# Cross attention of 32 batches on one core: warm-up products, two places of preparation work, and the last block of the output are changed

## The chip, the cores and the metric

The kernel runs on one core of a Trainium2 chip. The core has a matrix engine (TensorE, **PE** in the profile, with its weight loads as PEld), a vector engine (VectorE, **DVE**), a scalar engine (ScalarE, **ACT**), a general engine (GpSimd, **POOL**) and SyncE (**SP**), which here only issues transfers. PE writes its results into eight banks of PSUM (128 partitions by 512 floats each); everything else lies in SBUF. The metric is the device time of one execution, in microseconds; lower is better. The profile numbers times from the start of its span.

## What is computed

Inputs are x and y (32 batches of 256 channels by 1024 positions, float32), two weights of 256 by 256 for the energies and the values (`w_qk`, `w_v`), one for the output (`w_t`), and two biases. In the reference's words:

```python
x_q = jnp.einsum('oc,bcn->bno', w_qk, y)
x_k = jnp.einsum('oc,bcn->bon', w_qk, x)
x_v = jnp.einsum('oc,bcn->bon', w_v, x) + b_v[None, :, None]
energy = jnp.einsum('bnc,bcm->bnm', x_q, x_k)
attention = jax.nn.softmax(energy, axis=-1)
attention = attention / (1e-07 + attention.sum(axis=1, keepdims=True))
x_r = jnp.einsum('bcn,bnm->bcm', x_v, attention)
x_r = jax.nn.relu(jnp.einsum('oc,bcn->bon', w_t, x - x_r) + b_t[None, :, None])
return x + x_r
```

## The kernel before

**Weights are folded first.** Energies need only G = w_qk' w_qk, so the kernel makes G once (`pg`, line 169), multiplies it with x of a batch (`Keys`, tile `gx`) and that with y (`Energy`, tiles `pe`, `e`). The values take W = (w_t w_v)' with a minus sign: w_t is turned by four transposes on PE into the banks `pt` (line 179), copied to `wtT` by ACT, and multiplied with w_v into `pw` (line 184); `Values` multiplies x of a batch with the result into the tile `ut`. The bias of the values is a row `uc` = -(w_t b_v), made by `value_bias` (line 189): two copies on DVE (line 194) spread b_v over 128 columns (`bvb`), and PE multiplies them with wtT into `pb`. The same function has DVE make `fold`, a matrix for summing over positions, in four copies of 32 partitions (line 202).

**Every large product is a Strassen-like scheme of seven products.** `lefts` (line 145) prepares the left factors of a 256 by 256 weight: two ACT copies out of the banks and four sums on DVE (`gs`, `wtTs`, `wvtTs`). `summed` (line 218) prepares the right factors of x and y (`xs`, `ys`): for batch 0 with four POOL additions each, for later batches with accumulating transfers on POOL's queue, handed out as `steps`. `Seven` (line 245) holds the order of the seven products: p1, p5, p2, p6, p3, p7, p4, accumulated in three banks, with ACT copies in between and the four result blocks c11, c12, c22, c21 made by DVE (c21 by ACT). `Keys.factors` makes four more sums on POOL (`gt`), `Values.factors` another four (`us`). p4 adds into the bank from which c22 reads, so p4 waits for c22.

**A batch** is: for four tiles of 128 rows the seven energy products, with minima and maxima folded into the DVE instructions that make `e`, the exponentials on ACT, and sums over rows on DVE (`acc`); then the keys and values of the next batch; then the column sums (`part`, `pS`, `rc`) and the output (`Attention`). `Attention.run` (line 510) scales `e` (`normal`), makes the sums `et` of its quarters (`mix`; t1, t2, t3, t4) and runs the products in its order; `put` (line 490) adds x to a finished block and stores it; the block (1,0) is finished by ACT's relu, a DVE addition and a store (`c21`, line 497). The last products of a batch (`end`) are run inside the next batch's energies.

**Order.** `InOrder` (line 66) makes the calls that go through `pe`, `dve`, `act` and `pool` issue in the order in which the program makes them on that engine. Calls that go to `nc.vector`, `nc.scalar` or `nc.tensor` directly (in the head: the memset, the zero products, `lefts`, `value_weights`, `value_bias`) are placed by the framework's scheduler. [...]Transfers are issued by SP in the program's order, except the two biases (ACT's queue, lines 133 and 134) and the accumulating ones (POOL's).

**The head** (lines 129 to 143, 595 to 631): SP loads w_qk, x of batch 0, w_t, w_v and y; PE runs three products of zeros, 128 by 512, into a bank that nobody reads (lines 138 to 142), then G, then the keys of batch 0, w_t's turning, pw, pb, p4 of the keys, and the values of batch 0 through p4 (lines 617 to 628), and then the first energies.

**The tail** is the last batch's `run` with `before` set, and `finish` (line 553), which makes the last block in two halves of 256 columns: product, relu on ACT, addition on DVE, store, each half after the other.

Of the kernel before, what the change touches and what calls it, by code (L numbers as in the profile page):

```python
# [16 lines left out]
def kernel(  # L17
# [29 lines left out]
    nc = tc.nc  # L47
# [81 lines left out]
    nc.sync.dma_start(wqk, w_qk.rearrange("(k p) c -> p k c", p=P))  # L129
    load("x", 0, KC)  # L130
    nc.sync.dma_start(wt, w_t.rearrange("(k p) c -> p k c", p=P))
    nc.sync.dma_start(wv, w_v.rearrange("(k p) c -> p k c", p=P))
    nc.scalar.dma_start(bv, b_v.rearrange("(k p o) -> p k o", p=P, o=1))
    nc.scalar.dma_start(bt, b_t.rearrange("(k p o) -> p k o", p=P, o=1))
    load("y", 0)


    zeros = const.tile([P, MB], F32, name="zeros")
    nc.vector.memset(zeros, 0.0)
    idle = bank("idle")  # L140
    for _ in range(3):
        nc.tensor.matmul(idle, zeros[:, :P], zeros, start=True, stop=True)  # L142
    make_identity(nc, ident)

    def lefts(name, ps, sign=1.0):


        w = const.tile([P, KC, C], F32, name=name)
        for k in range(KC):
            nc.scalar.mul(w[:, k, :], ps[k][:, :C], sign)  # L150
        sums = const.tile([P, 4, P], F32, name=f"{name}s")
        s1, s2, s3, s4 = (sums[:, j] for j in range(4))

        def stt(out_, block, factor, other, op):
            nc.vector.scalar_tensor_tensor(out_, block, factor * sign, other, ALU.mult, op)

        p11, p12, p21 = ps[0][:, :P], ps[1][:, :P], ps[0][:, P:C]
        a11, a12, a21, a22 = w[:, 0, :P], w[:, 1, :P], w[:, 0, P:], w[:, 1, P:]
        stt(s1, p21, 1.0, a22, ALU.subtract)
        stt(s3, p11, 1.0, a21, ALU.subtract)  # L160
        stt(s2, p11, -1.0, s1, ALU.add)
        stt(s4, p12, 1.0, s2, ALU.add)
        return w, (a11, a12, s4, a22, s1, s2, s3)
# [2 lines left out]
    pg = [bank(f"pg_{i}") for i in range(KC)]  # L166
    for i in range(KC):
        for k in range(KC):
            nc.tensor.matmul(  # L169
                pg[i][:, :C], wqk[:, k, ts(i, P)], wqk[:, k, :], start=(k == 0), stop=(k == KC - 1)  # L170
            )
    _, g_left = lefts("g", pg, -1.0)

    def value_weights():

        pt = [bank(f"pt_{i}") for i in range(KC)]
        for i in range(KC):
            for k in range(KC):
                nc.tensor.transpose(pt[i][:, ts(k, P)], wt[:, k, ts(i, P)], ident)
        wtT, t_left = lefts("wtT", pt)  # L180
        pw = [bank(f"pw_{i}") for i in range(KC)]
        for i in range(KC):
            for k in range(KC):
                nc.tensor.matmul(  # L184
                    pw[i][:, :C], wv[:, k, ts(i, P)], wtT[:, k, :], start=(k == 0), stop=(k == KC - 1)
                )
        return wtT, t_left, lefts("wvtT", pw, -1.0)[1]

    def value_bias(wtT):

        bvb = scratch[:, 6, : KC * P].rearrange("p (k c) -> p k c", k=KC)
        pb = bank("pb")
        for k in range(KC):
            nc.vector.tensor_copy(bvb[:, k, :], bv[:, k, :].to_broadcast([P, P]))
            nc.tensor.matmul(  # L195
                pb[:, :C], bvb[:, k, :], wtT[:, k, :], start=(k == 0), stop=(k == KC - 1)
            )
        nc.scalar.mul(uc[:, 0, :], pb[:, :C], -1.0)
        nc.scalar.mul(nbt[:, :, 0], bt[:, :, 0], -1.0)

        for a in range(NG):
            nc.vector.tensor_copy(
                fold[ts(a, G32)],
                ident[ts(a, G32), ts(a, G32)].unsqueeze(1).to_broadcast([G32, NG, G32]),
            )
# [6 lines left out]
    def temp(tag, name):  # L212
        return cp.tile([P, MB], F32, tag=tag, name=name)
# [221 lines left out]
    class Attention(Seven):  # L435
# [27 lines left out]
                into, t_left[j - 1], self.xr[j - 1], start=not onto, stop=False, skip_group_check=True  # L463
            )

        def epart(self, into, j, tiles=range(HT), cols=slice(0, MB)):
            for t in tiles:
                pe.matmul(
                    into[:, cols],
                    self.ur[j - 1][:, t],  # L470
                    self.er[j - 1][:, t, cols],
                    start=False,
                    stop=(t == HT - 1),
                    skip_group_check=True,
                )
# [34 lines left out]
        def run(self, u, before=None):  # L510


            self.normal(0, 0)
            if u:
                u.c22()
            self.normal(1, 0)
            if before:
                before.put()
                before.c21()
            self.normal(0, 1)  # L520
            self.mix(self.t1, self.b11, self.b12, ALU.add)
            self.normal(1, 1)
            self.mix(self.t2, self.t1, self.b22, ALU.subtract)
            self.epart(self.one, 1)
            self.p1s = self.biased(self.one, "p1s", bt[:, 0, :])
            self.epart(self.three, 2)
            self.epart(self.two, 5)
            self.p5s = self.biased(self.two, "p5s", bt[:, 1, :])
            self.xpart(self.one, 6, True)
            if u:  # L530
                u.p4()
                u.c21()
                u.c11()
                u.c12()
            self.c11()
            self.put()
            self.xpart(self.two, 3, True)
            self.epart(self.two, 3, (0, 1))
            self.epart(self.one, 6)
            self.w = self.biased(self.one, "w", nbt[:, 0, :])  # L540
            self.mix(self.t3, self.b12, self.b22, ALU.subtract)
            self.mix(self.t4, self.b21, self.t2, ALU.subtract)
            self.epart(self.two, 3, (2,))
            if u:
                self.epart(self.two, 3, (3,))
                self.c12()
                self.put()
# [4 lines left out]

        def finish(self):

            self.xpart(self.one, 7, True)
            self.epart(self.one, 7)
            self.epart(self.two, 3, (3,))
            self.c22()
            self.put()
            self.c12()  # L560
            self.put()
            self.xpart(self.one, 4, True)
            z = temp("z", f"z_{self.b}_1_0")
            for cols in (ts(0, MB // 2), ts(1, MB // 2)):
                self.epart(self.one, 4, cols=cols)
                act.activation(
                    z[:, cols], self.one[:, cols], AF.Relu, bias=bt[:, 1, :], scale=1.0
                )
                dve.tensor_tensor(
                    z[:, cols], z[:, cols], loaded["x", self.b][:, 1, cols], ALU.add  # L570
                )
                nc.sync.dma_start(out[self.b, ts(1, P), cols], z[:, cols])

    def columns(b):

# [24 lines left out]
    g.p2()  # L600
    g.c11()
    g.p6()
    g.p3()
    g.c12()
    g.p7()
    g.c22()
    wtT, t_left, u_left = value_weights()
    value_bias(wtT)
    g.p4()
    g.c21()  # L610
# [13 lines left out]
    u.c12()  # L624
    u.p7()
    u.c22()
    u.p4()
    u.c21()
    u.bias()
    xsteps[1]()  # L630
    xsteps[2]()

    before = None
    for b in range(B):
# [3 lines left out]
        for t in range(HT):  # L638
            now = Energy(b, t, lhs, rhs)
            pair.append(now)  # L640
            now.p1()
            if t > 0:
                pair[t - 1].exp(1)
            now.p5()
            if t == 0:
                if before is not None and more:
                    before.end()
                    before.c21()
                    load("x", b + 1)
                e = ep.tile([P, NT, N], F32, tag="e", name=f"e_{b}")  # L650
                acc = one.tile([P, N], F32, tag="acc", name=f"acc_{b}")
                ur, usteps = u.factors()
            if t > 1:
                pair[t - 2].share(0)
            if t == 0:
                now.p6()
            now.p2()
            now.c11()
            if t == 1:
                pair[0].scale(1)  # L660
            if t > 1:
                pair[t - 1].share(1)
            if t > 0:
                now.p6()
            if t == 1:
                act.activation(acc, e[:, HT, :], AF.Copy, scale=scales[HT])
            if t > 0:
                pair[t - 1].p4()
                pair[t - 1].c21()
                pair[t - 1].exp(0)  # L670
            now.p3()
            now.c12()
            now.p7()
            now.c22()
            if t == 0:
                for step in usteps:
                    step()
                if more and b > 0:
                    xn, xsteps = summed("x", b + 1)
            elif more and b > 0:  # L680
                xsteps[t - 1]()
# [100 lines left out]
```

## Time and profile before

| what | value |
|---|---|
| median of 3 runs | 2153.83 us (2153.35 to 2154.16) |
| the profiled execution | 2153.93 us |
| its span | 2152.1 us |
| one batch in the steady state (start of the energies to the next) | 66.56 us |
| PE products of the head: zeros, from 1.45 us | G from 6.73, keys from 8.62, values from 18.60, energies from 25.94 |
| last product's first pass | 2142.81 us |
| DVE's last instruction | 2148.76 us, 0.42 us long |
| DMA | 131 GB/s on average over the span |

A float32 product appears in the profile as two records on PE, so "x8" are four products. [...]one of 512 columns lasts 592 ns, yet the next starts 0.43 us after it. The busy shares of the page are averages over 32 batches; the change touches only the first 30 us and the last 35, so the timeline of these windows is what to read. In a timeline the brackets at a line's end give the idle time of the engine before it and what ended it.

### The profile page before, as it was taken

How to read it: one execution, taken by the hardware profiler on the slowest of the kernel's cores; microseconds unless marked ns; L12 is line 12 of the kernel's file. 1: busy time of each engine (PE TensorE's matmuls, PEld its weight loads, DVE VectorE, ACT ScalarE, POOL GpSimd, SP SyncE). 2: the span in 40 equal slices, each digit the busy share in tenths (PEclk: the TensorE clock that was granted, in tenths of full speed). 3: DMA queues.
4: the chain of work that ended last, by engine and by line, in shares of the span. 5: the costliest groups of instructions: out<-in, count | busy, mean ns of one | idle time of the engine just before them, and what ended most of it. 6: DMA issues, size and time to landing. Idle time of an engine off the chain costs nothing.

```text
span 2152.1 us, 19871 instructions
## 1 busy us (share of the span) xinstructions
PE 2143.6 (100%) x6374; PEld 1064.0 (49%) x6374; DVE 1803.4 (84%) x2964; ACT 788.5 (37%) x1322; POOL 597.4 (28%) x488
## 2 busy tenths in 40 slices
PE   9999999999999999999999999999999999999998
PEld 5555445555445545455544555545554445544453
DVE  5898888898888988889888898888888888988897
ACT  4224432344432344323443234442244422444332
POOL 4322223322233223232232321323222233222320
PEclk9999999999999999999999999999999999999999
DMA  6555665556655556665566654665546655566640
GB/s 157 132 123 122 151 156 123 123 122 150 149 123 134 118 144 147 127 144 110 137 149 134 143 114 126 157 144 129 128 117 150 154 123 129 119 149 147 126 94 30
DMA packets 139192, 282.59 MB, mean 131 GB/s; under 512 B 9168, under 2 KB 42960, under 8 KB 139088
## 3 DMA queue, kind: packets, MB, share of 16 engines
q0 software_dynamic: 75936, 114.83, 33.9%
q1 hardware_dynamic: 62608, 166.48, 22.6%
q8 instruction: 51, 0.84, 0.2%
q14 instruction: 53, 0.43, 0.1%
q10 hardware_dynamic: 544, 0.00, 0.0%
HBM read 181.67 MB, written 33.55 MB: 100 GB/s over the span
## 4 chain that ended last, share of the span: by engine, by line
PE 98%; DVE 1%; issue 0%; ACT 0%; DVEq 0%
PE po L77 44%; PE pe L77 35%; PE pu L77 9%; PE pg L77 9%; DVE e L77 1%; PE idle L142 0%; DVE acc L77 0%; PE pS L77 0%; PE pw L184 0%; PE pg L169 0%; DVE z L77 0%; DVE rc L77 0%; DVE et L77 0%; ACT z L77 0%; PE pb L195 0%
## 5 line engine op out<-in xcount | busy, mean ns | idle before, releaser
L77 PE MATMUL pe<-gt,ys 128*128 128x512 f32 x768 | 392.2, 592 | 0.0
L77 DVE SCALAR_TENSOR_TENSOR e<-e,ri,rc 128x512 f32<-128x512 f32 x512 | 348.6, 743 | 1.1
L77 PE MATMUL po<-et,us 128*128 128x512 f32 x768 | 345.4, 592 | 1.2 <-DVE et L77 1.2
L77 DVE SCALAR_TENSOR_TENSOR acc<-e,ri,acc 128x1024 f32<-128x1024 f32 x224 | 288.9, 1290 | 8.0
L77 PE MATMUL pe<-gx,y 128*128 128x512 f32 x512 | 261.4, 592 | 0.0
L77 DVE TENSOR_TENSOR et<-e 128x1024 f32<-128x1024 f32 x128 | 254.0, 2022 | 0.0
L77 PEld LDWEIGHTS pe<-gt,ys 128*128 128x128 f32 x768 | 145.8, 190 | 184.2 <-issue 178.4
L77 PEld LDWEIGHTS po<-et,us 128*128 128x128 f32 x768 | 144.3, 190 | 187.0 <-issue 186.1
L77 PE MATMUL po<-e,ut 128*128 128x512 f32 x512 | 224.9, 593 | 0.0
L77 POOL TENSOR_TENSOR gt<-gx 128x512 f32<-128x512 f32 x64 | 101.7, 1589 | 433.2 <-DVE gx L77 433.2
L77 ACT COPY ep1s<-pe 128x512 f32<-128x512 f32 x128 | 75.0, 586 | 301.8 <-PE pe L77 285.1
L77 ACT ACTIVATE e<-e,nm 128x1024 f32<-128x1024 f32 x128 | 147.1, 1149 | 98.5 <-DVE nm L77 97.0
L77 PEld LDWEIGHTS po<-e,ut 128*128 128x128 f32 x512 | 97.3, 190 | 122.5 <-issue 94.5
L77 PEld LDWEIGHTS pe<-gx,y 128*128 128x128 f32 x512 | 97.2, 190 | 122.0 <-issue 114.1
L77 DVE CUSTOM_DVE_ANT_0 e<-pe,ep1s 128x512 f32<-128x512 f32 x128 | 88.5, 691 | 78.9 <-ACT e L77 62.8
L77 DVE TENSOR_TENSOR z<-z,x 128x512 f32<-128x512 f32 (+1 forms) x33 | 22.3, 676 | 149.7 <-ACT z L77 149.7
L77 ACT ACTIVATE e<-e,bias 128x1024 f32<-128x1024 f32 x128 | 147.4, 1151 | 0.5 <-DVE bias L77 0.5
L77 POOL DMA_DIRECT2D ut<-uc x32 | 50.5, 1579 | 313.2 <-DVE ut L77 258.3
L77 PE MATMUL pe<-gx,ys 128*128 128x512 f32 x256 | 130.9, 593 | 0.4 <-DVE nm L77 0.4
L77 PE MATMUL pe<-gt,y 128*128 128x512 f32 x256 | 130.7, 592 | 0.0
L77 POOL TENSOR_TENSOR us<-ut 128x512 f32<-128x512 f32 x64 | 82.6, 1291 | 149.1 <-DMA ut<-uc 149.1
L77 PE MATMUL po<-e,us 128*128 128x512 f32 x256 | 120.5, 592 | 0.0
(112 smaller groups left out, 3250.1 us busy)
## 6 DMA issues: line engine op xcount, KB each, us to landing
y<-in_ctx_dram SPq DMA_DIRECT2D x32, 1024.0 KB, 4.9
ut<-uc POOLq DMA_DIRECT2D x32, 1024.0 KB, 9.7
out_dram<-z SPq DMA_DIRECT2D x127, 256.0 KB, 2.0
x<-in_x_dram SPq DMA_DIRECT2D x31, 1024.0 KB, 8.2
xs<-in_x_dram SPq DMA_DIRECT2D x62, 512.0 KB, 4.4
ys<-in_ctx_dram SPq DMA_DIRECT2D x62, 512.0 KB, 4.1
xs<-in_x_dram POOLq DMA_DIRECT2D x31, 512.0 KB, 9.1
xs<-xs POOLq DMA_DIRECT2D x31, 512.0 KB, 5.0
```

Of the source, the lines that this page charges most:

```text
L77: self.last = getattr(self.engine, name)(*args, **kwargs)
```

## The change

It does five things.

- The products of zeros become eight of 128 by 128, on a tile `few` of their own, cleared ahead of `zeros`.
- The two bias loads go to SP's queue: b_v between w_t and w_v, b_t between w_v and y.
- w_t's turning (`turned_weights`) is split from `value_weights` and stands between p6 and p3 of batch 0's keys; the copies that spread b_v (`spread_bias`) stand behind the keys' c22; `fold` stays in `value_bias`. All of this now goes through the ordered `pe`, `dve` and `act`, so that its place is the program's.
- p4 and c21 of batch 0's values, their bias transfer and two steps of batch 1's `xs` go behind the first two energy products of batch 0.
- In the last batch the previous batch's last `put` and `c21` go behind the sum t1, and the last block is made whole: one product sequence of 512 columns, one DVE instruction max(z, -b_t) + (x + b_t) that takes the bank, and one store. x + b_t is made earlier by ACT.

On the engines' queues this leaves the number of products the same except for the zeros (three become eight) and the last block (eight of 256 columns become four of 512).

```diff
     nc.sync.dma_start(wt, w_t.rearrange("(k p) c -> p k c", p=P))
+    nc.sync.dma_start(bv, b_v.rearrange("(k p o) -> p k o", p=P, o=1))
     nc.sync.dma_start(wv, w_v.rearrange("(k p) c -> p k c", p=P))
-    nc.scalar.dma_start(bv, b_v.rearrange("(k p o) -> p k o", p=P, o=1))
-    nc.scalar.dma_start(bt, b_t.rearrange("(k p o) -> p k o", p=P, o=1))
+    nc.sync.dma_start(bt, b_t.rearrange("(k p o) -> p k o", p=P, o=1))
     load("y", 0)
...
     zeros = const.tile([P, MB], F32, name="zeros")
-    nc.vector.memset(zeros, 0.0)
+    few = const.tile([P, P], F32, name="few")
+    dve.memset(few, 0.0)
+    dve.memset(zeros, 0.0)
     idle = bank("idle")
-    for _ in range(3):
-        nc.tensor.matmul(idle, zeros[:, :P], zeros, start=True, stop=True)
+    for _ in range(8):
+        pe.matmul(idle[:, :P], few, few, start=True, stop=True)
...
-    def value_weights():
+    def turned_weights():
 
         pt = [bank(f"pt_{i}") for i in range(KC)]
         for i in range(KC):
             for k in range(KC):
-                nc.tensor.transpose(pt[i][:, ts(k, P)], wt[:, k, ts(i, P)], ident)
-        wtT, t_left = lefts("wtT", pt)
+                pe.transpose(pt[i][:, ts(k, P)], wt[:, k, ts(i, P)], ident)
+        return lefts("wtT", pt)
+
+    def value_weights(wtT):
+
         pw = [bank(f"pw_{i}") for i in range(KC)]
...
+    def spread_bias():
+        for k in range(KC):
+            dve.tensor_copy(bvb[:, k, :], bv[:, k, :].to_broadcast([P, P]))
...
             self.normal(1, 0)
+            self.normal(0, 1)
+            self.mix(self.t1, self.b11, self.b12, ALU.add)
             if before:
                 before.put()
                 before.c21()
-            self.normal(0, 1)
-            self.mix(self.t1, self.b11, self.b12, ALU.add)
...
         def finish(self):
 
+            xb = temp("op1s", f"xb_{self.b}")
+            act.activation(
+                xb, loaded["x", self.b][:, 1, ts(0, MB)], AF.Identity, bias=bt[:, 1, :], scale=1.0
+            )
...
-            self.xpart(self.one, 4, True)
+            self.end()
             z = temp("z", f"z_{self.b}_1_0")
-            for cols in (ts(0, MB // 2), ts(1, MB // 2)):
-                self.epart(self.one, 4, cols=cols)
-                act.activation(
-                    z[:, cols], self.one[:, cols], AF.Relu, bias=bt[:, 1, :], scale=1.0
-                )
-                dve.tensor_tensor(
-                    z[:, cols], z[:, cols], loaded["x", self.b][:, 1, cols], ALU.add
-                )
-                nc.sync.dma_start(out[self.b, ts(1, P), cols], z[:, cols])
+            dve.scalar_tensor_tensor(z, self.one, nbt[:, 1, :], xb, ALU.max, ALU.add)
+            self.store(1, 0, z)
...
     g.p6()
+    wtT, t_left = turned_weights()
     g.p3()
     g.c12()
     g.p7()
     g.c22()
-    wtT, t_left, u_left = value_weights()
+    spread_bias()
+    u_left = value_weights(wtT)
     value_bias(wtT)
...
-    u.p4()
-    u.c21()
-    u.bias()
-    xsteps[1]()
-    xsteps[2]()
...
             if t == 0:
-                if before is not None and more:
+                if b == 0:
+                    u.p4()
+                    u.c21()
+                    u.bias()
+                    xsteps[1]()
+                    xsteps[2]()
+                elif more:
                     before.end()
```

More of the change, by code (lines that the diff above doesn't have):

```diff
@@ L149, in lefts @@
         for k in range(KC):
-            nc.scalar.mul(w[:, k, :], ps[k][:, :C], sign)
+            act.mul(w[:, k, :], ps[k][:, :C], sign)
         sums = const.tile([P, 4, P], F32, name=f"{name}s")
@@ L154, in stt @@
         def stt(out_, block, factor, other, op):
-            nc.vector.scalar_tensor_tensor(out_, block, factor * sign, other, ALU.mult, op)
+            dve.scalar_tensor_tensor(out_, block, factor * sign, other, ALU.mult, op)
         p11, p12, p21 = ps[0][:, :P], ps[1][:, :P], ps[0][:, P:C]
@@ L168 @@
         for k in range(KC):
-            nc.tensor.matmul(
+            pe.matmul(
                 pg[i][:, :C], wqk[:, k, ts(i, P)], wqk[:, k, :], start=(k == 0), stop=(k == KC - 1)
@@ L183, in value_weights @@
             for k in range(KC):
-                nc.tensor.matmul(
+                pe.matmul(
                     pw[i][:, :C], wv[:, k, ts(i, P)], wtT[:, k, :], start=(k == 0), stop=(k == KC - 1)
                 )
-        return wtT, t_left, lefts("wvtT", pw, -1.0)[1]
+        return lefts("wvtT", pw, -1.0)[1]
+    bvb = scratch[:, 6, : KC * P].rearrange("p (k c) -> p k c", k=KC)
+    def spread_bias():
+        for k in range(KC):
+            dve.tensor_copy(bvb[:, k, :], bv[:, k, :].to_broadcast([P, P]))
     def value_bias(wtT):
-        bvb = scratch[:, 6, : KC * P].rearrange("p (k c) -> p k c", k=KC)
         pb = bank("pb")
         for k in range(KC):
-            nc.vector.tensor_copy(bvb[:, k, :], bv[:, k, :].to_broadcast([P, P]))
-            nc.tensor.matmul(
+            pe.matmul(
                 pb[:, :C], bvb[:, k, :], wtT[:, k, :], start=(k == 0), stop=(k == KC - 1)
             )
-        nc.scalar.mul(uc[:, 0, :], pb[:, :C], -1.0)
-        nc.scalar.mul(nbt[:, :, 0], bt[:, :, 0], -1.0)
+        act.mul(uc[:, 0, :], pb[:, :C], -1.0)
+        act.mul(nbt[:, :, 0], bt[:, :, 0], -1.0)
         for a in range(NG):
-            nc.vector.tensor_copy(
+            dve.tensor_copy(
                 fold[ts(a, G32)],
@@ L464, in xpart, with epart @@
             )
-        def epart(self, into, j, tiles=range(HT), cols=slice(0, MB)):
+        def epart(self, into, j, tiles=range(HT)):
             for t in tiles:
                 pe.matmul(
-                    into[:, cols],
+                    into,
                     self.ur[j - 1][:, t],
-                    self.er[j - 1][:, t, cols],
+                    self.er[j - 1][:, t],
                     start=False,
```

## The prediction

> **What bounds the kernel now.** I read the page's head and its chain of waits first. The span is 2152.1 us of the profiled execution's 2153.93 us; the runs' median is 2153.83, so the sum below is made in the span and moved over unchanged (0.1 us apart).
>
> ```profile
> span 2152.1 us, 19871 instructions
> PE 2143.6 (100%) x6374; PEld 1064.0 (49%) x6374; DVE 1803.4 (84%) x2964; ACT 788.5 (37%) x1322; POOL 597.4 (28%) x488
> PE 98%; DVE 1%; issue 0%; ACT 0%; DVEq 0%
> ```
>
> PE carries the whole chain. Thirty of the 32 batches are untouched and repeat every 66.56 us, so the change can win only where PE stands or runs slowly: before batch 0's energies and in batch 31's tail. First the tail, in the chain by time (start, length, what), and the timeline behind its last part (start, length, engine, idle before it):
>
> ```profile
> 2115.99 4.72 DVE e L77 x7
> 2120.71 1.20 DVE z L77 x2
> 2121.91 1.39 DVE e L77 x3
> ...
> 2124.57 1.15 DVE et L77
> 2125.71 0.14 issue
> 2125.85 19.83 PE po L77 x48
> ```
> ```profile
> 2142.81 1.12 PE L77 MATMUL po<-xs,wtT 128*128 128x512 f32 x2
> 2143.77 1.89 PE L77 MATMUL po<-et,ut 128*128 128x256 f32 x8
> 2146.22 1.99 PE L77 MATMUL po<-et,ut 128*128 128x256 f32 x8 [0.56 <-ACT z L77]
> ```
>
> Read: two z instructions of DVE lie on the path to the sum (et) that PE awaits, and the second half of the last block waits for ACT to read the first. Now the head: the timeline of PE, then the groups by tile (count: ns min/median/max, first to last start):
>
> ```profile
> 15.04 1.99 PE L184 MATMUL pw<-wtT,scratch 128*128 128x256 f32 x8 [0.25 <-ACT wtT L150]
> 24.94 1.16 PE L77 MATMUL pu<-wvtT,xs 128*128 128x128 f32 x8 [0.78 <-DVE ut L77]
> ```
> ```profile
> L142 PE MATMUL idle<-zeros x6: 1061/1061/1219, 1.5 to 5.9; 128*128 128x512 f32 x6
> L202 DVE COPY fold<-scratch x4: 218/1093/1283, 9.8 to 12.5; 32x128 f32<-32x128 f32 x4
> L194 DVE COPY scratch<-scratch x2: 221/224/227, 4.8 to 5.0; 128x128 f32<-128x128 f32 x2
> ```
>
> Read: a product is two records (passes). The zero passes start 0.853 us apart and last 1061 ns; the same form lasts 592 ns later: they run at half clock. PE waits for wtT and for ut. And the fold copies last five times as long as the like-sized bias copies of line 194, which ran while POOL was idle.
>
> **The tail.** (1) The two z instructions (1.20 us) move behind the sum t1. PE's product before it is through at 2124.46 (last start 2124.04 + 0.43), t1's first half would be there 1.20 us earlier, so PE starts at 2124.65 instead of 2125.85: **1.20 us**. DVE's total stays, so t2 still ends at 2129.40 + 2.35 = 2131.75; PE wants its first half at 2133.04 - 1.20 = 2131.84. Tight, but met; t3 (2135.35, wanted at 2137.17) has room. (2) The last block whole: from 2142.81 to the end of DVE's last instruction (2148.76 + 0.42) are 6.37 us. After: 0.96 to the first pass of e, 8 passes at 0.43, 0.16 for the last one's end, then one instruction out of the bank, 0.69 by the z row of that shape: 5.26 us. Saves 1.11. Its store is 256 KB (2.0 us to landing in the page) instead of 128 KB (1.7): -0.27. The added x + bias on ACT lies in the 8.3 us in which ACT idles before its last relu. Tail: 1.20 + 0.84 = **2.0 us** (1.5 to 2.2, if the store lands as slowly as the 2.3 of the last window, or as fast as 1.7).
>
> **The head, to the first product.** The first memset shrinks from 512 to 128 columns: from 0.485 us to between 0.20 (POOL's of that size) and 0.485; I take 0.28, so PE starts at 1.24 instead of 1.45. Sixteen passes of a quarter of 0.853 us take 3.41; with 0.16 of filling they end at 4.81. w_qk lands at 0.74 + 3.9 = 4.64, so PE does not stand. G's products thus start 1.92 us earlier than 6.73, but still cold: their starts (6.73, 7.11, 7.33) put the switch to full clock at about 7.05. Five and a quarter of the eight passes run at 0.427 instead of 0.216; they end at 7.64 instead of 8.62: **0.98**. Here a rule weighs. The Trainium skill (TensorE: Matmul & The Clock Gate, Part 1: The HAM clock gate) says that full clock comes after a window of about 3.4 us of sustained activity, at a phase of its own. The row shows 5.6 us from first pass to switch; the rule would allow 3.4 to 6.8. By the row the gain is 0.98, by the rule's earliest switch about 1.9. I keep the row. The b_v and b_t loads leave ACT's queue for SP's (0.49 and 0.50 us to issue); w_v, y and x of batch 1 issue up to 1 us later behind them, but y's packets had waited for the DMA engines anyway (issued 3.65, landed 12.4), so nothing.
>
> **w_t's turning** goes between p6 and p3. Before, from its first pass to pw's were 0.85 us, 0.41 of them waiting for ACT's wtT; now p3 and p7 (1.7 us) cover that: **0.45** with the small wait in p7. DVE now does wtT's sums ahead of c12 and c22. pb could start at 16.88 - 1.43 = 15.45.
>
> **The bias copies are the doubtful step.** They move from 4.81, where they cost nothing, to behind c22, so to about 15.0 on DVE; pb waits for them, and p4, the values and everything on PE behind pb. POOL runs ys and gt there without a gap from 12.43 to 22.54, 1.24 us each. Row: with POOL idle such a copy takes 224 ns; the fold copies beside POOL took 1093 to 1283, each ending when POOL's instruction ended. The rule that speaks against the change is the Trainium skill's (SBUF — State Buffer, Who interferes with whom): DVE copies in two-port mode and POOL lock each other out for a whole instruction. By the idle row, pb starts at 15.45 and the head gains 2.6; by the rule and the fold rows the first copy waits half an instruction (0.62) and the second, as POOL stands ready again, a whole one: 15.0 + 0.62 + 1.24 + 0.2 = 17.05, pb at 17.2. That is 0.35 later than before, and eats all of the 1.43. I take this, since the fourth fold copy, issued right behind the third, let POOL's ys in between. The fold copies themselves come after wvtT's sums, from 18.1 to at most 23.2, when POOL's stream ends; c11, c12, c22 of u follow by 25.0.
>
> **The values' last product** goes behind the energies' first two. Before, PE stood from 24.00 to 24.94 for c22, and 0.13 for ACT ahead of the energies' third product. From u's first product to the energies' third were 9.19 us, now 5.40 + 1.72 + 0.90 = 8.02: **1.17**; it is wanted at 26.1, c22 is there at 25.0. What pays: u's copy on ACT now follows two energy copies, so the bias DMA on POOL, and behind it in POOL's queue xs's two steps and the four us instructions, come at 40.5 instead of 39.7, while PE is 0.8 earlier. DVE's sums (acc) meet these: 1.44 and 2.21 us instead of 1.28, and DVE has no slack from 40.1 to 51.3 by the chain. Relative to them us moves by 1.6 us: between -1.1 (none meets) and +1.3 (two sums wait a whole POOL instruction); I take **-0.4**, nearer to what is there.
>
> **Sum.** Head: -0.35 + 1.17 - 0.4 = 0.4. Tail 2.0. Total 2.4 us: span 2149.7, **time 2151.4 us**.
>
> **Rivals.** *The copies slip in* (0.27): both get in at one boundary or meet none; pb at 15.5 to 16. Head 1.7 to 2.6, total 3.7 to 4.6: about 2149.6. For it: 224 ns at 4.81; against: the fold rows. *The clock comes a window late* (0.10): the shorter zeros leave a hole before w_qk or count for less; full clock at 10.4 instead of 7.05 costs half of 3.4 us: 2153.1. Against: PE is busy without a hole by the sum. *POOL keeps the port* (0.10), the slower side: at 2076.93 one et sum of DVE lasted 4533 ns where its twin took 1210, waiting over both of POOL's gt instructions in a row. If a copy loses at every boundary, pb waits for the stream's end, 22.6: values 5.8 us late, head -4.6, total -2.6: 2156.5, more if PE cools down. It decides from the fourth boundary lost (two more cost 2.7 us); against it: each fold copy got in at the next boundary. *The ends don't bring it* (0.05): t2 late or the store slow, tail 0.8: 2152.6.
>
> **Chances and range.** Forecast 0.48. The measurement tells from no change about 0.2%, 4.3 us, that is times below 2149.5 or above 2158.1. Faster beyond it needs the free copies and more: 0.20; slower beyond it needs the kept port and a cold PE: 0.04; the rest 0.76. The range, 2149.0 to 2153.3, leaves out the kept port and the extreme of the free copies.
>
> **What would show it.** Zero passes ending near 4.8 and G's first passes still 0.43 apart; pb's start (15.5 or 17.2) and DVE's two copies before it (0.2 or over 1 us each); no wait of u's last product for ut; the et wait at 2125.85 gone; one last store, DVE ending 5.3 us after the last block's first pass. I am wrong if pb waits not at all, or if the energies' first stall, 0.17 us at 51.37 before, grows beyond 1 us.

## The result, and the profile after

The changed kernel takes **2149.82 us** (median of 20 runs, 2147.97 to 2150.94), the kernel before on the same chips 2153.76 us (20 runs, 2152.73 to 2154.33): a ratio of 0.9982, 95% interval 0.9975 to 0.9989, or 3.9 us. The forecast was 2151.4, with a range from 2149.0 to 2153.3. What the forecast did not have is the spread: 3.0 us over the runs of the changed kernel, 1.6 over those of the one before. The experiments had to explain that too.

The profiled execution took 2150.47 us, its span is 2148.7. The head of the page, and the line of the chain's shares by engine:

```profile
span 2148.7 us, 19867 instructions
PE 2141.6 (100%) x6376; PEld 1063.8 (50%) x6376; DVE 1806.6 (84%) x2964; ACT 788.0 (37%) x1321; POOL 597.4 (28%) x488
PE 98%; DVE 1%; DMA 0%; issue 0%; POOL 0%; ACT 0%; SPq 0%; DVEq 0%; POOLq 0%
```

Nothing changes in the large, as the steady batches are the same; but DMA and POOL, which were not in the old chain's shares, are in this one. The chain of the first 30 us says where (start, length, what):

```profile
1.73 6.56 DMA x<-in_x_dram
...
8.43 1.28 POOL xs L77
...
9.75 1.14 PE pg L77 x2
...
14.37 2.22 DVE scratch L77 x2
16.59 0.04 issue
16.63 0.70 PE pb L77 x2
17.33 0.86 PE pg L77 x2
18.19 5.41 PE pu L77 x48
23.59 1.72 PE pe L77 x4
25.31 0.89 PE pu L77 x8
26.20 3.86 PE pe L77 x9
```

The head is now held at two places: x's second half with POOL's sum of it ends just ahead of the keys' p6 (9.75), and DVE's two bias copies, 2.22 us of them, end just ahead of pb (16.63). The keys' p4 (17.17) stands behind pb in PE's queue and so begins behind it, though it uses nothing of pb, and c22, for which it has to wait, ended at 14.37. Ahead of the energies' third product nothing waits any more: four passes, the values' last product (eight), and on. The same in the timeline of PE (start, length, operation; in brackets PE's idle time and what ended it):

```profile
1.05 3.79 PE L77 MATMUL idle<-few 128*128 128x128 f32 x16 [1.05 <-DVE few L77]
4.63 2.15 PE L77 MATMUL pg<-scratch 128*128 128x256 f32 x8
6.62 1.02 PE L77 MATMUL pg<-x,g 128*128 128x512 f32 x2
...
15.41 0.70 PE L77 MATMUL pb<-wtT,scratch 128*128 128x256 f32 x2 [0.65 <-DVE scratch L77]
16.63 0.70 PE L77 MATMUL pb<-wtT,scratch 128*128 128x256 f32 x2 [0.52 <-DVE scratch L77]
```

And in the tail, the timeline of PE and then that of all engines:

```profile
2123.02 3.67 PE L77 MATMUL po<-et,us 128*128 128x512 f32 x8
```
```profile
2144.64 0.75 DVE L77 SCALAR_TENSOR_TENSOR z<-po,nbt,xb 128x512 f32<-128x512 f32 x1 [2.66 <-PE po L77]
2145.42 0.33 SPq L492 DMA_DIRECT2D out_dram<-z  x1
```

PE starts on `et` without a bracket, that is without waiting, and one DVE instruction and one store end the kernel.

For the next table, G in PE's timeline before:

```profile
6.73 2.05 PE L169 MATMUL pg<-scratch 128*128 128x256 f32 x8
```

How far the changed kernel is ahead of the old one, at points of the two profiles:

| point | before | after | ahead by |
|---|---|---|---|
| G's first pass | 6.73 | 4.63 | 2.10 |
| keys' p1 (G is through) | 8.62 | 6.62 | 2.00 |
| keys' p6 | 11.47 | 9.75 | 1.72 |
| pw | 15.04 | 12.87 | 2.17 |
| values' p1 | 18.60 | 18.03 | 0.57 |
| energies' p6 | 27.78 | 26.04 | 1.74 |
| first pass of pS, batch 0 | 59.33 | 57.68 | 1.65 |
| first pass of pS, last batch | 2113.09 | 2111.46 | 1.63 |
| end of the last z on DVE | 2149.19 | 2145.39 | 3.80 |
| end of the span | 2152.1 | 2148.7 | 3.4 |

The head brings 1.65 us of this, the tail 1.8.

### The profile page after: what moved, and what is told of

It is laid out like the page before. It is cut to its first block, busy times and chain, and to the rows that moved or that the text cites. A ratio compares the mean times of both kernels' runs of the same rounds, so it can differ in the third digit from the quotient of the medians.

```text
span 2148.7 us, 19867 instructions
## 1 busy us (share of the span) xinstructions
PE 2141.6 (100%) x6376; PEld 1063.8 (50%) x6376; DVE 1806.6 (84%) x2964; ACT 788.0 (37%) x1321; POOL 597.4 (28%) x488
## 4 chain that ended last, share of the span: by engine, by line
PE 98%; DVE 1%; DMA 0%; issue 0%; POOL 0%; ACT 0%; SPq 0%; DVEq 0%; POOLq 0%
PE po L77 45%; PE pe L77 35%; PE pu L77 9%; PE pg L77 9%; DVE e L77 0%; DMA x<-in_x_dram 0%; DVE acc L77 0%; PE pS L77 0%; DVE scratch L77 0%; POOL xs L77 0%; DVE gx L77 0%; DVE wtTs L77 0%; DVE z L77 0%; PE pb L77 0%; ACT gw L77 0%
## 5 line engine op out<-in xcount | busy, mean ns | idle before, releaser
L77 DVE TENSOR_TENSOR z<-z,x 128x512 f32<-128x512 f32 x31 | 21.5, 693 | 145.7 <-ACT z L77 145.7
```

The source lines that it names most:

```text
L77: self.last = getattr(self.engine, name)(*args, **kwargs)
```

## The experiments

Theory: the zeros and the point at which PE's rate doubles set when G is through; DVE's bias copies take turns with POOL; each part of the tail is worth what it was priced at. Rival theories stand in each expectation, mostly of the form "something else holds this place anyway". Each kernel is the changed one with the edit shown. The profiles also serve as repeated samples of what was not edited. In the text, g and u are the keys and the values of batch 0, and "u's p1" is the first product of the values. Experiments 3 to 7 ran once each, so only stretches of their profiles are read, not their times.

Two things were not tried: the bias loads back in ACT's queue, and DVE's copies at their old early place. There they took 0.36 us at 4.81, as soon as b_v had landed (4.0 us after its issue at 0.74) and with POOL idle; in the changed kernel b_v lands 6.6 us after its issue at 2.68.

**1. The bias copies on ACT.**

```diff
-            dve.tensor_copy(bvb[:, k, :], bv[:, k, :].to_broadcast([P, P]))
+            act.copy(bvb[:, k, :], bv[:, k, :].to_broadcast([P, P]))
```

> The changed kernel with the two bias copies made by ACT in place of DVE, nothing else. Theory (DVE's two copies, 14.29 to 16.58 in the changed kernel, take turns with POOL's sums of y, and PE's pb stands behind them): ACT's copies run at some 0.3 to 0.4 us each whatever POOL does, pb follows pw at once at about 14.6 instead of 15.41 and 16.63, the keys' p4 begins at about 15.7 instead of 17.17, and the start of every later stage moves by 1.4 to 1.6 us: pS at about 56.4, span about 2147.2, if the granted clock rises at the same point as in the changed kernel's profile. Rival (POOL's sums for y and the keys hold the first energies anyway, so the wait only moves): p4 is early, but the first energy e.p6 stays within 0.3 us of 26.04 and the span of 2148.7.

2148.37 us (7 runs, 2147.39 to 2148.75; ratio to before 0.9974, 0.9963 to 0.9985), span 2146.4. Group and timeline of that profile:

```profile
L77 ACT COPY scratch<-scratch x2: 308/314/319, 11.6 to 11.8; 128x128 f32<-128x128 f32 x2
```
```profile
12.56 1.89 PE L77 MATMUL pw<-wtT,scratch 128*128 128x256 f32 x8
14.29 1.03 PE L77 MATMUL pb<-wtT,scratch 128*128 128x256 f32 x4
15.15 1.02 PE L77 MATMUL pg<-xs,g 128*128 128x512 f32 x2
16.01 1.05 PE L77 MATMUL pu<-wvtT,x 128*128 128x128 f32 x8
```

ACT makes a copy in 0.31 us, pb follows pw with no bracket, and from pw's first pass to the values' p1 are 3.45 us instead of 5.16: 1.71 for the copies. The values, energies and pS all keep it; the rival falls. In this profile ACT makes the copies between 11.62 and 12.13, while POOL is idle until 13.90; that ACT is not held up beside POOL is shown by experiments 8 and 9 alone, where its copies run beside POOL's sums of y and take 0.29 to 0.30 us each. In 8:

```profile
11.80 1.27 POOL L77 TENSOR_TENSOR ys<-y 128x512 f32<-128x512 f32 x1 [0.57 <-DMA y<-in_ctx_dram]
12.20 0.50 ACT L77 COPY scratch<-scratch 128x128 f32<-128x128 f32 x2 [0.57 <-DMA scratch<-in_L_xattn_b_v_dram]
```

By pS this kernel is 2.30 ahead of the profile after: 0.31 of that came before pw (POOL's sum of x began 0.51 earlier, and p6 0.20), 1.71 from the copies, and 0.28 later, from a stall in the energies that is missing here.

**2. The old zeros.** Three products of 512 columns again:

```diff
-    few = const.tile([P, P], F32, name="few")
-    dve.memset(few, 0.0)
...
-    for _ in range(8):
-        pe.matmul(idle[:, :P], few, few, start=True, stop=True)
+    for _ in range(3):
+        pe.matmul(idle, zeros[:, :P], zeros, start=True, stop=True)
```

> The changed kernel with the kernel before's three products of 512 zero columns in place of the eight of 128, nothing else. Theory (the end of the zeros and the clock's rise set where G ends): G begins at about 6.7 instead of 4.63 and ends at 7.6 to 8.6 instead of 6.62, by where the granted clock rises; p6 no longer waits for POOL's sum and begins at 10.4 to 11.5 instead of 9.75, and 0.7 to 1.7 us are left of that at pS (58.5 to 59.5). Rival (the head's gain comes from w_t's turning and the loads, not from the zeros, since POOL's second sum of x holds p6 in any case): p6 moves by less than 0.4 us, and pS stays within 0.4 us of 57.85.

2151.66 us (10 runs; ratio 0.999, 0.9981 to 1.0). G begins at 6.30, ends at 8.03, p6 is at 10.88, pS at 58.34, 0.66 later than after. Against the kernel before on its own chip this one gains 2.0 us, the changed kernel 3.9: by the medians the zeros are worth 1.9, about half of the whole. The two intervals overlap, but eight of the ten runs lie above all twenty of the changed kernel. The rival falls on p6 (1.13 later, not under 0.4); pS lies between what theory and rival said for it, since this profile's copies cost 0.37 less.

Experiments 3 to 6 undo one part of the change each.

**3. The z steps at their old place.**

```diff
+            if before:
+                before.put()
+                before.c21()
             self.normal(0, 1)
             self.mix(self.t1, self.b11, self.b12, ALU.add)
-            if before:
-                before.put()
-                before.c21()
```

> The changed kernel with the last stage's two z steps of the batch before put back ahead of the second normalisation and the sum t1, nothing else. Theory: PE waits again for et in the last stage's second product, 1.2 us, so that the stretch from pS of the last batch to the last DVE instruction is 1.2 us longer (34.9 instead of 33.7) and the span with it. Rival (DVE has the same work in either order, so its end decides): within 0.3 us of 33.7.

The wait is back at its old length:

```profile
2123.23 3.67 PE L77 MATMUL po<-et,us 128*128 128x512 f32 x8 [1.21 <-DVE et L77]
```

From the first pass of pS, last batch, to the end of the last z: 35.13 us, against 33.93 in every other kernel with the whole last block made by one instruction. 1.20, as priced.

**4. The values' last product at its old place**, ahead of the energies.

```diff
     u.c22()
+    u.p4()
+    u.c21()
+    u.bias()
...
-                if b == 0:
-                    u.p4()
-                    u.c21()
-                    u.bias()
...
-                elif more:
+                if b > 0 and more:
```

> The changed kernel with the values' last product and what follows it put back ahead of batch 0's energies, nothing else. Theory: the product stands again for DVE's c22 (about 0.9 us) and the energies' third product again for ACT: from u's first product to the energies' p6 9.1 to 9.2 us instead of 8.01. POOL's bias DMA comes earlier again, so that the later sums of DVE meet the four us instructions elsewhere; if that cost the 0.4 us that was set down for it, the stretch from u's first product to pS grows by 0.8 only, and if nothing, by 1.17 (the two profiles at hand say 1.08: 40.73 before, 39.65 after).

From u's first product to the energies' p6: 9.19 instead of 8.01, with the old wait in PE's timeline:

```profile
22.79 1.16 PE L77 MATMUL pu<-wvtT,xs 128*128 128x128 f32 x8 [0.78 <-DVE ut L77]
```

1.18, as priced. To pS it grows by 1.70, more than either number expected: the stall of PE ahead of the last energies' p4 is 0.78 us here (0.17 before, 0.33 after). The step that I feared for POOL's later instructions goes the other way in this profile; in the twelve profiles with the new place that stall is 0.28 to 0.35 us nine times and missing three times.

**5. The last block in two halves**, as before.

```diff
-            self.end()
+            self.xpart(self.one, 4, True)
...
-            dve.scalar_tensor_tensor(z, self.one, nbt[:, 1, :], xb, ALU.max, ALU.add)
-            self.store(1, 0, z)
+            for cols in (ts(0, MB // 2), ts(1, MB // 2)):
+                self.epart(self.one, 4, cols=cols)
...
```

> The changed kernel with the last block again in two halves, each with its relu on ACT, its sum on DVE and its store, nothing else. Theory: the second half's products stand for ACT's read of the first half, 0.5 us, and relu and sum follow one after the other: from pS of the last batch to the end of DVE's last instruction 37.8 instead of 36.73 us; the last store is 128 KB instead of 256 KB and its end follows DVE's by 0.4 us less, so the span grows by 0.6 to 0.7 only against the same head. Rival (the store's size costs nothing): the span grows by the full 1.0.

In that expectation two scales are mixed: 36.73 reaches from pS to a point 0.5 us ahead of the span's end, not to the last z, which ends 33.93 behind pS. By the z, 34.89: 0.96 longer. By the span's end, 37.87 instead of 37.23: 0.64 longer. So the whole block saves 0.96 and its store, with twice the bytes, gives 0.33 back (3.31 us from z's end to the span's end instead of 2.98); the rival falls. Below, "the end" is the span's; the 36.5 to 36.7 of later expectations are 0.5 less for the same thing, and their 3.25 is 0.05 less.

**6. w_t's turning behind p7.**

```diff
-    wtT, t_left = turned_weights()
     g.p3()
     g.c12()
     g.p7()
     g.c22()
+    wtT, t_left = turned_weights()
     spread_bias()
```

> The changed kernel with w_t's turning put back behind p7, nothing else. Theory: from p6 to pw 3.57 us instead of 3.12 (PE stands for ACT's wtT), but pb's start is set by DVE's two bias copies, which come free where POOL's sums of y end; so those 0.45 us are hidden there, and u's first product comes at most 0.2 us later than the same POOL times give it. Rival (the turning's place is worth its 0.45 to the end): pw, pb, p4 and u's first product are all 0.45 later against POOL's ys.

p6 to pw: 3.57, as in the kernel before, instead of 3.12 in the changed kernel's profile. There the second pass of p6 came 0.10 late; in 2, 3, 4 and 7, where p6 did not stand for POOL, it is 3.01 to 3.02. So the place is worth 0.55, where 0.45 was priced. But the next wait is not that much later:

```profile
12.55 1.99 PE L77 MATMUL pw<-wtT,scratch 128*128 128x256 f32 x8 [0.25 <-ACT wtT L77]
14.71 1.13 PE L77 MATMUL pb<-wtT,scratch 128*128 128x256 f32 x4 [0.16 <-DVE scratch L77]
```

pb waits for the copies, and those for POOL: POOL's first sum of y begins at 13.30 and u's first product 3.24 later; in experiment 4, with the new turning, 13.21 and 3.23. In such an execution the turning's gain is eaten by the copies.

**7. The bias loads behind y.**

```diff
-    nc.sync.dma_start(bv, b_v.rearrange("(k p o) -> p k o", p=P, o=1))
...
-    nc.sync.dma_start(bt, b_t.rearrange("(k p o) -> p k o", p=P, o=1))
     load("y", 0)
+    nc.sync.dma_start(bv, b_v.rearrange("(k p o) -> p k o", p=P, o=1))
+    nc.sync.dma_start(bt, b_t.rearrange("(k p o) -> p k o", p=P, o=1))
```

> The changed kernel with the loads of b_v and b_t behind y in the same queue, nothing else. If the 4-byte packets of the two bias loads slow x's second half (DMA moved 155 to 300 GB/s while they ran), x lands at 7.5 to 7.9 instead of 8.29, POOL's second sum begins that much earlier and p6 at about 9.1 to 9.4 instead of 9.75; the bias then lands later, and pb may wait for it. If the loads share the queues by size alone, x lands within 0.2 us of 8.29 and p6 stays at 9.75.

POOL's second sum of x began at 7.47 and p6 at 9.20, which looked like a hit. Two more kernels with late loads (8 and 9 below) had it at 7.50 and 8.60, the ten with early loads at 6.35 to 8.43. So one profile had misled: the loads' place does not show on x. y's first sum began at 11.35, 11.80 and 12.47 with late loads and at 12.09 to 14.41 with early ones; so it may show on y, but that was not tried further.

**What the profiles show together.** POOL's first sum of y, the copies and the stretch from pw to u's first product, in the seven kernels whose copies are on DVE behind c22:

| profile | POOL's first sum of y from | first copy from | both copies take | pw to u's p1 |
|---|---|---|---|---|
| after | 12.66 | 14.29 | 2.29 | 5.16 |
| 2 | 12.09 | 15.31 | 1.92 | 4.79 |
| 7 | 11.35 | 13.63 | 1.63 | 4.50 |
| 4 | 13.21 | 13.67 | 1.02 | 4.18 |
| 6 | 13.30 | 13.81 | 0.98 | 3.99 |
| 3 | 13.81 | 14.72 | 0.57 | 3.73 |
| 5 | 14.41 | 13.76 | 0.36 | 3.52 |
| six with ACT's copies | 11.80 to 13.90 | | | 3.45 |

The two ends of this table in the timeline of all engines, the changed kernel first, then experiment 5:

```profile
14.01 1.27 POOL L77 TENSOR_TENSOR ys<-y,ys 128x512 f32<-128x512 f32 x1
14.29 2.29 DVE L77 COPY scratch<-scratch 128x128 f32<-128x128 f32 x2
...
15.23 1.26 POOL L77 TENSOR_TENSOR ys<-y 128x512 f32<-128x512 f32 x1
...
16.45 1.27 POOL L77 TENSOR_TENSOR ys<-y,ys 128x512 f32<-128x512 f32 x1
```
```profile
13.76 0.36 DVE L77 COPY scratch<-scratch 128x128 f32<-128x128 f32 x2
...
14.41 1.27 POOL L77 TENSOR_TENSOR ys<-y 128x512 f32<-128x512 f32 x1 [2.78 <-DMA y<-in_ctx_dram]
```

The same two instructions take 0.36 us when POOL is still waiting for y, and 2.29 when it is at work: in the changed kernel's profile the first ends 0.08 us behind POOL's second sum, the second 0.08 us behind its third. In 3, 4 and 6 the copies met y's first sum; POOL's next one depends on it (1.35 us from start to start instead of 1.22), and both copies got in at that one end. So where the copies fall among POOL's sums decides between 0.07 and 1.7 us, and that is set by when y lands and when DVE comes to them, without any edit of either.

The second thing left to chance is G. The zeros and G are the same in the changed kernel and in experiments 3 and 5. The changed kernel's G is shown above; PE's timeline in experiment 3, then in 5:

```profile
4.63 2.98 PE L77 MATMUL pg<-scratch 128*128 128x256 f32 x8
```
```profile
4.40 1.89 PE L77 MATMUL pg<-scratch 128*128 128x256 f32 x8
```

Eight passes take 2.98, 2.15 or 1.89 us: their starts are 0.43 us apart until the rate doubles, and 0.216 after it. Worked out from those starts, the doubling comes 3.1 to 5.8 us after PE's first pass in the fourteen profiles (before 5.6, after 4.1); both ends of that, 5.8 in 3 and 3.1 in 5, belong to kernels with the same head. The traces' records of the granted clock say the same: in all fourteen the record of the full clock begins at that very point (7.05 before, 5.15 after, 6.82 in 3, 4.15 in 5). Ahead of it a trace holds no clock record, and a table by windows prints 1.00 there all the same, since it counts time without a record as full clock. The records of full clock last 2143.57 us or 2140.16, which are 628 and 627 times 3.4133. This fits a raster of 3.413 us on which the rate changes, and whose place against the kernel's start differs from execution to execution.

With the copies on ACT, in six sets of 7 to 11 runs, the spread is 1.4 to 1.9 us, against 3.0 over 20 runs of the changed kernel and 2.7 over the 10 runs of experiment 2. So the copies are likely a good part of the spread that the forecast did not have, and the draw of G another.

**8 to 12. Combinations**, all with the copies on ACT (experiment 1). In **8**, late bias loads (experiment 7), and:

```diff
-    for _ in range(8):
+    for _ in range(6):
...
+    wtT, t_left = turned_weights()
     g.p6()
-    wtT, t_left = turned_weights()
     g.p3()
```

> The changed kernel with four edits of the head: bias copies on ACT, loads of b_v and b_t behind y, w_t's turning ahead of p6, and six products of zeros instead of eight. By the theory: w_qk lands at 3.5, so G begins at about 3.8 instead of 4.63; where the granted clock rises (4.6 to 6.9 in the profiles so far) half of that 0.8 is kept, G ends at 5.9 to 7.0; x's second half lands at about 7.5, the turning covers POOL's second sum, p6 begins at 9.2 to 9.8 (0.43 of turning ahead of it); pb follows pw at once; u's first product at 15.0 to 16.0 (16.01 with the copies on ACT alone), pS of batch 0 at 54.5 to 55.4, span 2145.4 to 2146.4, median 0.5 to 1.0 us under the 2148.4 of ACT's copies alone. Rival (with fewer zeros PE's clock rises later, or the bias now lands too late): no better than 2148.4.

2148.54 us (10 runs, ratio 0.9977): the rival's side. G began at 3.78 as expected, but the rate doubled late (5.1 us after the first pass), and the turning ahead of p6 cost 0.15 us of small waits in p3 and p7 and covered nothing.

In **9**, one edit at each end: late loads, and the last instruction and store in halves:

```diff
-            dve.scalar_tensor_tensor(z, self.one, nbt[:, 1, :], xb, ALU.max, ALU.add)
-            self.store(1, 0, z)
+            h = MB // 2
+            for eng, c in ((nc.sync, slice(0, h)), (nc.scalar, slice(h, MB))):
+                dve.scalar_tensor_tensor(
+                    z[:, c], self.one[:, c], nbt[:, 1, :], xb[:, c], ALU.max, ALU.add
+                )
+                eng.dma_start(out[self.b, ts(1, P), c], z[:, c])
```

> Bias copies on ACT and, against that kernel, two edits at the two ends, each read off its own stretch: the loads of b_v and b_t behind y, and the last block's DVE instruction in two halves, each with its own store, in two queues (SP's and ACT's). Head: if the 4-byte packets slow x, POOL's second sum begins at 7.4 to 7.6 again (7.9 to 8.4 in five of seven profiles with these loads ahead of y, 6.3 and 6.6 in the two others), so that p6 never waits, and y's sums begin at 11.3 to 11.8 (12.1 to 14.4). If not, these times scatter as before. Tail: the first half's store leaves 0.3 us earlier and the second moves 128 KB, so from the last z's end to the program's end 2.9 instead of 3.25 us, z itself ends 0.1 later; from pS of the last batch to the end 36.5 instead of 36.73. Rival (a second queue's store lands later): 36.7 or more. Median 2147.8 to 2148.3 by the first, against the 2148.4 of ACT's copies alone.

2148.75 us (11 runs, ratio 0.9979). x's sum began at 8.60: the theory of the loads fell here. The tail, 37.10 instead of 37.23 from pS to the end, gains half of what was expected; z ends 0.12 later and from there to the end it takes 3.04 instead of 3.30.

In **10**, six zeros, and two stores of the whole z:

```diff
-            self.store(1, 0, z)
+            h = MB // 2
+            nc.sync.dma_start(out[self.b, ts(1, P), ts(0, h)], z[:, :h])
+            nc.scalar.dma_start(out[self.b, ts(1, P), ts(1, h)], z[:, h:])
```

> Bias copies on ACT and, against that kernel, two edits at the two ends, each read off its own stretch: six products of zeros instead of eight, and the last block's store in two stores of 128 KB from the whole z, in two queues. Head: G begins at 3.8 instead of 4.63; by where the granted clock rises (4.15 to 6.9 so far) G ends at 5.5 to 7.0 instead of 6.1 to 7.4, on the mean 0.4 earlier; but where G ends early, p6 stands for POOL's second sum of x. Median 0 to 0.4 below the kernel with ACT's copies alone. Tail: two stores side by side: 0.0 to 0.3 less than 36.73 from pS to the end.

2148.12 us (11 runs, ratio 0.9977). G ended at 6.30; the two stores cost 0.11 (37.35 from pS to the end).

In **11**, six zeros (as in 10) and the halves (as in 9), and beside it in **12** the first experiment's kernel again:

> The changed kernel with what paid or cost nothing so far: bias copies on ACT, six products of zeros, and the last block's instruction and store in two halves. G begins at 3.8 instead of 4.63 and is through at 5.5 to 7.0, by where the clock rises; pb follows pw without a wait (1.73 us from pw's first pass to pb's); pS of the last batch to the end 36.6 instead of 36.73. Median: the 2148.1 of the kernel with two whole stores less 0.24 for the tail, 2147.9; 0.3 to 0.6 below ACT's copies alone on the same chip. Rival (the six products give only what the clock's rise leaves to chance): within 0.3 of ACT's copies alone.

2147.63 us (7 runs, 2146.54 to 2148.27; ratio 0.9973, 0.9963 to 0.9984), tail 37.10 again, G from 3.78 to 6.69.

> The kernel with the bias copies on ACT alone a second time, beside the combination on one chip: median 2148.2 to 2148.6, and a spread over the runs of about 1.4 us, half of the changed kernel's 3.0, since the clock's rise is left of its two chances and the turns of DVE and POOL are gone. Profile: from pw's first pass to u's first product 3.45 us again; the clock's rise anywhere between 4.1 and 6.9.

2148.75 us (11 runs, ratio 0.9978, 0.9969 to 0.9987), 3.45 again from pw to u's p1. The median is 0.15 above what was expected, and the spread is 1.9 us, not 1.4. The combination is the fastest kernel of the study, 5.8 us below the kernel before on its chip against 3.9 for the change. Beside ACT's copies alone on the same chip it is 1.1 us faster, more than expected; against experiment 1, each by its own kernel before, 0.4. The tail gives 0.13 of that. The intervals overlap, so what the six zeros add is likely and not settled.

## Why the prediction came out as it did

**The tail held.** The z order 1.20 against 1.20; the whole last block 0.96 against 1.11; its store -0.33 against -0.27. In sum 1.83 against 2.0. The block came out smaller since its last instruction took 0.75 us where the z row of that shape said 0.69, and starts 0.26 us behind the last pass by PE's spacing (2143.95 and 0.43 on), not 0.16.

**The head, to the first product, is the mis-sized term: 0.98 was forecast, 2.00 measured.** Its parts: G began at 4.63, not at 4.81, for the smaller memset took 0.17 us and not 0.28, and began 0.09 earlier. But the larger part is "I keep the row": the prediction put the doubling of PE's rate at 7.05, where the old profile had it, and at 5.15 it came. That row was one draw. The rule beside it, the Trainium skill (TensorE: Matmul & The Clock Gate, Part 1: The HAM clock gate), had a phase of its own and, as an estimate made from it, a span from 3.4 to 6.8 us; the fourteen profiles have 3.1 to 5.8. The rule's form was right, and its window agrees with the raster of 3.413 us; the kernel before happened to sit near its late end (5.6), and the row should have been read as that. Of the 2.00, 0.28 was lost again at p6, to x and POOL, which the prediction did not see.

**w_t's turning** brought 0.45 up to pw in this profile, and 0.55 where p6 does not wait; how much of it remains is up to the copies (experiment 6).

**The bias copies** were rightly the doubtful step, and the mechanism was right: DVE's copy waits for the end of POOL's instruction, as the Trainium skill said (SBUF — State Buffer, Who interferes with whom); that POOL waits for DVE in turn, as that section also has it, these runs do not show. The first pb was forecast for 17.2 and began at 15.41, its second half, behind the second copy, at 16.63; of the 2.17 us that pw was ahead, 1.60 were gone at u's first product, where the forecast lost 1.78. But it is a draw and not a fixed cost: 0.07 to 1.7 us over seven profiles, by where the copies fall among POOL's sums. The rival "the copies slip in", with its 0.27, is what experiment 5 showed in full and 3, 4 and 6 in part. The profile that answers the forecast so well is the dearest of the seven; that is luck.

**The values' last product**: 1.17 forecast, 1.17 measured. **The meeting with POOL's later instructions** was set down at -0.4; the lead shrank by 0.1 from the energies to pS.

**The sum** was 2.4 for 3.4 in the profiles and 3.9 in the medians. In the profiles G brought 1.0 more than forecast, the meeting with POOL cost 0.3 less and the copies 0.2 less, while p6 took 0.3 and the tail gave 0.2 less. The rest lies in the draws: the profile before was 0.2 above its median, the one after 0.65. That the copies cost less in the median run than in the profile is likely by the seven profiles, but no profile of a median run shows it. The measured 2149.8 also lies next to the 2149.6 of the rival "the copies slip in", but not by its cause: in the profile the copies did take turns, and G made up for it. The rivals that lost: the rate never came a window late (at the latest at 6.82, not 10.4), POOL held the two copies over no more than two of its instructions in any profile, the ends brought what they were to.

## What to carry to other kernels

A stretch at the start of a kernel is one draw of things that have no fixed phase, here the doubling of PE's rate and the landing of a load: look at it in several executions before pricing an edit from it. For a short copy that PE waits for, an engine that takes a little longer but always the same can be better than one that is faster only when it is not held up: here ACT's 0.29 to 0.32 us in six profiles beat DVE's 0.21 to 1.3 in seven. And undoing a change part by part showed that three of its parts (the zeros, the z order and the values' last product, 1.2 to 1.9 us each) carried most of the gain, while the copies' move had a cost that a single profile may miss altogether.

## What was not expected of the hardware

- PE's rate doubles between 3.1 and 5.8 us after its first pass, from execution to execution, at points that fit a raster of 3.413 us. The trace's clock record begins only there; the 1.00 that a table by windows prints ahead of it is no reading.
- Two DVE copies of 128 by 128 take 0.36 us with POOL idle and up to 2.29 beside it; both got in at one end of a POOL instruction when POOL's next depended on it (1.35 us from start to start), one when it did not (1.22).
- DVE's sums that read a bank (`wvtTs`, 0.27 to 0.29 us) ran beside POOL's without such a delay.
- Loads issued in the same order land up to 2 us apart between executions: POOL's sum of x's second half began at 6.35 to 8.43 us with the same queue.
- A store of 256 KB in place of 128 KB costs 0.33 us at the end of the kernel; the same 256 KB from two queues at once costs 0.11 more than from one, and in two halves, each behind its own instruction, 0.13 less.
